# Macaron block on one core: attention and down weights loaded in parts, weight sums of the first block moved to GpSimd

## The chip, the cores and the metric

One core of a Trainium2 chip. The metric is the device time of one execution in microseconds (us); lower is better. Its engines are named as in the profile: PE (TensorE), DVE (VectorE), ACT (ScalarE), POOL (GpSimd) and SP (SyncE, which issues all DMAs of this kernel). A letter q behind an engine's name means its instruction queue.

## What is computed

The input `x` has 8 batches of 512 tokens of 512 features, all in float32. Each batch goes through a feed-forward stage, an attention stage and a second feed-forward stage with the same weights. The feed-forward stage keeps the two largest of every four hidden values.

```python
def _L0_ffn_ref(x, w_gate, w_up, w_down):
    h = silu(x @ w_gate) * (x @ w_up)      # 512 -> 2048
    h_sparse = _sparsify_2to4(h)           # two largest magnitudes of four stay
    return h_sparse @ w_down               # 2048 -> 512

x = x + 0.5 * _L0_ffn_ref(_layernorm(x), w_gate, w_up, w_down)
x = x + _L0_attn_ref(_layernorm(x), W_q, W_k, W_v, W_o)   # 16 heads, 4 of keys and values, rotary
x = x + 0.5 * _L0_ffn_ref(_layernorm(x), w_gate, w_up, w_down)
```

## The kernel before

**Blocks.** A block is one feed-forward stage of one batch; there are 16 of them, in an order that lets a batch's attention run beside the blocks of others. One block has four chunks of hidden values (`c`), each with two groups (`i`, 0 to 7). A group computes a quarter of a chunk's gate and up values.

**Products with sums of quarters.** A group's weights come as quarters of 256 KB: Q11, Q12, Q21, Q22. All groups but the first of the first block are done by seven products instead of eight (`woven`, L613 on): some take a quarter, others a sum of quarters S1 to S4 (S1 = Q21 + Q22, S2 = S1 - Q11, S3 = Q11 - Q21, S4 = Q12 - S2). The order in a group is Q11, S1, S2, S4, S3, Q12, Q22. The products that belong together collect in three PSUM banks x, v and z. ScalarE or VectorE copies what is there to `row` and `corner`; VectorE adds the later parts (L638), and a product into x must wait until VectorE has read x for `corner`. The last product of each group (`x<-ts,w`, Q22) is such a one: TensorE waits there if the add to `corner` is late.

**Sums of gate and up.** The sums do not change from block to block. The first block makes them (`combine_gu`, L688): for group i + 1 they are recorded after the third product of group i, four instructions on VectorE (L693) through a queue of work that may wait (`for_later`). Each sum is also stored to DRAM (L694), from where later blocks load it (L116).

**Mask.** After each chunk, VectorE makes the mask of two of four in two halves (`keep_two_of_four`, L393 on): L414, L416, L418, L419 compare magnitudes that ScalarE made (L401), eight bf16 steps L423 to L435 count, four L440 multiply the mask into `h`. GpSimd then makes sums of quarters of `h` (L446 after the first half; L448 to L451 after the second).

**Down.** Two chunks make a pair (`g`, 0 and 1). Each pair has seven products with the down weights (`products`, L532 on), in the order of the table PRODUCTS at L476: `11`, `11+12`, `22`, `21+22`, `11+22` and so on. Those that need sums of quarters of `w_down` load them from DRAM (L513), those that don't load from the input (L517). The sums are made in the first block by GpSimd (`combine_down`, L492 on): per chunk one load `raw` of 1 MB (L496), then five sums (L505), each stored (L506).

**Attention** (`attention`, L772 on) loads its weights `wqkv` (L776), the rotary tables `cs` (L780) and, later, `wo` (L830). It runs as a generator beside the feed-forward blocks: each `yield` is a step. It starts with `layernorm_t` (L278 on), which loads the rows `xn` (L286), makes their statistics on VectorE (L292), scales on GpSimd (L299 to L307), applies them on ScalarE (L310) and transposes on TensorE (L262).

**Order.** The program is written out in one order, and each engine carries out its own instructions in that order. A planner decides the order while the program is built: it keeps an estimated time for TensorE, VectorE and ScalarE (`at`), puts VectorE work that is not urgent where its estimate says that VectorE has room (`fill`), and advances the side stages (attention, layernorm, `combine_down`) when they are due by a table (`sides`, L1003): start, end, steps. GpSimd and the DMA queue have no estimate. All DMAs go through SP's queue, in order; a DMA that waits for an engine or for a free buffer holds those behind it. At most eight are under way: each waits for the eighth before it.

The lines that matter most:

```python
            raw = p_slots.tile([P, 4, D], FP, "raw")                       # L495
            nc.sync.dma_start(out=raw, in_=w_down[c])
            there = at["pe"] + 12.0
...
            def one(j, a, b, op):                                           # L692
                nc.vector.tensor_tensor(w[j], a, b, op)
                nc.sync.dma_start(out=gu_sums[i][:, j - S1], in_=w[j])
...
    sides = [(11, 18, 6, partial(combine_down, 0), None, None), (22, 32, 6, partial(combine_down, 1), None, None)]
```

Of the kernel before, what the change touches and what calls it, by code (L numbers as in the profile page):

```python
# [14 lines left out]
ALU = mybir.AluOpType  # L15
# [3 lines left out]
P = 128  # L19
# [7 lines left out]
def macaron_block(  # L27
# [12 lines left out]
    nc = tc.nc  # L40
    B, S, D = x.shape
    ND = D // P
    NT = S // P
    NCH = w_gu.shape[0]
    KV = N_KV * HD
# [27 lines left out]
    tokens = []  # L73
# [14 lines left out]
    Q11, Q12, Q22, Q21, S1, S2, S3, S4 = range(8)  # L88
# [52 lines left out]
    at = {"pe": 0.0, "dve": 0.0, "act": 0.0}  # L141
    urgent, put_off, for_later = deque(), deque(), deque()
# [33 lines left out]
    def waits(end):  # L176

        takes("pe", 0.0, end + TOLD)

    def later(us, does, ready=None, queue=put_off):  # L180
        queue.append(Later(us, does, pe_heard() if ready is None else ready, queue))
        return queue[-1]

    def soon(us, does, ready=None):

        return later(us, does, ready, urgent)
# [283 lines left out]
    gu_made, written = {}, {}  # L470
# [21 lines left out]
    def combine_down(g):  # L492

        for c in range(2 * g, 2 * g + 2):
            raw = p_slots.tile([P, 4, D], FP, "raw")  # L495
            nc.sync.dma_start(out=raw, in_=w_down[c])  # L496
            there = at["pe"] + 12.0
            yield lambda: there
            yield now
            quarter = {f"{i + 1}{j + 1}": raw[:, i::2, j * HD2 : (j + 1) * HD2] for i in range(2) for j in range(2)}  # L500
            sums = wa_slots.tile([P, 6, 2, HD2], FP, "sums")

            for i, name in enumerate(SUMS):
                op = ALU.add if name[2] == "+" else ALU.subtract
                nc.gpsimd.tensor_tensor(sums[:, i], quarter[name[:2]], quarter[name[3:]], op)  # L505
                nc.sync.dma_start(out=combined[g, name][:, c % 2 * 2 : c % 2 * 2 + 2, :], in_=sums[:, i])  # L506
            yield now
        done_down.add(g)
# [13 lines left out]
    def ffn(b, final, last):  # L522
# [165 lines left out]
        def combine_gu(i):  # L688

            w = [quarters[(b, final), i, q] for q in range(8)]  # L690

            def one(j, a, b, op):  # L692
                nc.vector.tensor_tensor(w[j], a, b, op)  # L693
                nc.sync.dma_start(out=gu_sums[i][:, j - S1], in_=w[j])  # L694

            gu_made[i] = [
                later(0.62, partial(one, j, w[a], w[b], op), at["pe"], for_later)
                for j, a, b, op in (
                    (S1, Q21, Q22, ALU.add),
                    (S2, S1, Q11, ALU.subtract),  # L700
                    (S3, Q11, Q21, ALU.subtract),
                    (S4, Q12, S2, ALU.subtract),
                )
            ]

        opens = (b, final) == blocks[0]
        hs, last_one = [], []
        for c in range(NCH):
# [27 lines left out]
            else:  # L736
                for pair in range(2):
                    i = 2 * c + pair
                    if opens and i == 0:
                        combine_gu(0)  # L740
                        groups = (g for r in range(2) for g in hidden(h, 0, r, slice(0, S)))
                        last_one = gu_made.pop(0)
                    else:
                        groups = woven(h, i, 2 * pair, last_one)
                    for k, g in enumerate(groups):
                        yield g
                        if k == 2 and opens and i + 1 < 2 * NCH:
                            combine_gu(i + 1)

                        if pair == 1 and c % 2 == 0 and k in (3, 4):  # L750
                            yield from some(1)
                    if opens:
                        load_quarters(*[key for key in quarters if key[:2] == ((b, final), i)])
                    if i == 2 * NCH - 1:
                        in_xT.remove(here)
                    if pair == 1:
                        begin(keep_two_of_four(h, list(last_one), e))
                        yield from some(5, False)
# [13 lines left out]
    def attention(b):  # L772
        ensure(written[b, 0])
        wa = wa_slots.tile([P, ND, D + 2 * KV], FP, "wqkv")
        for src, col in ((w_k, D), (w_q, 0), (w_v, D + KV)):
            nc.sync.dma_start(  # L776
                out=wa[:, :, col : col + src.shape[1]], in_=src.rearrange("(c p) n -> p c n", p=P)
            )
        cs = p_slots.tile([P, 4, S], FP, "cs")
        nc.sync.dma_start(out=cs[:, :2, :], in_=rope.rearrange("a p s -> p a s"))  # L780
        got = {}
        yield from layernorm_t(got, "xa", tokens[b][1])
        xT = got["xT"]
        qT = qkvp.tile([P, ND, S], FP, tag="qT", name="qT")
        kT = qkvp.tile([P, S], FP, tag="kT", name="kT")
# [29 lines left out]
        for t in range(NT):  # L815
            for k in range(ND):
                nc.tensor.matmul(  # L817
                    out=vps.tile[:, t, :],
# [8 lines left out]
        nc.scalar.copy(v, vps.tile)  # L827
        vps.free(end=takes("act", 0.6, pe_heard()))
        wo = wa_slots.tile([P, ND, D + 2 * KV], FP, "wo")
        nc.sync.dma_start(out=wo[:, :, :D], in_=w_o.rearrange("(c p) n -> p c n", p=P))  # L830
        yield partial(when, of_k + of_q[0])

        def scores(c, t, nm):

            sc = sc_slots.tile([P, N_KV, S], FP, "sc")
            waits(sc_slots.ready)
            for kv, rows in enumerate(heads):
                nc.tensor.matmul(  # L838
                    out=sc[:, kv, :], lhsT=qT[rows, c, t * P : (t + 1) * P], rhs=kT[rows, :], start=True, stop=True
                )  # L840
            multiplied(1.07, True)
            for kv in range(N_KV):
                one = partial(nc.vector.tensor_reduce, nm[:, t, kv : kv + 1], sc[:, kv, :], AX.X, ALU.max, negate=True)
                found = soon(0.6, one)
            return [sc_slots.used(found)]

        def in_pieces(nm):


            def pieces():  # L850
                nc.vector.tensor_copy(z[:, :, :, 0], nm)
                for i in (1, 2):
                    nc.vector.tensor_tensor(nm, nm, z[:, :, :, i - 1], ALU.subtract)
                    nc.vector.tensor_copy(z[:, :, :, i], nm)

            return [soon(1.15, pieces)]
# [63 lines left out]
        ensure(of_k + of_q[0])  # L920
        for t in range(NT):
            found = scores(0, t, nm)
            yield partial(when, found)
        pieces = in_pieces(nm)
        yield partial(when, pieces)
# [3 lines left out]
        p, sums = None, []  # L929
        for c in range(ND):  # L930
            waits(ensure(pieces))
            mT = pieces_by_row()
            there = [Done(at["act"])]
            nm = maxima()
            for t in range(NT):
# [15 lines left out]
                p = other if t else total  # L951
# [17 lines left out]
        for t, xt in enumerate(xts):  # L969
            y = Bank([P, D], "y")  # L970
            for k in range(ND):
                nc.tensor.matmul(  # L972
                    out=y.tile, lhsT=qT[:, k, t * P : (t + 1) * P], rhs=wo[:, k, :D], start=(k == 0), stop=(k == ND - 1)
# [26 lines left out]
        return WIDTH * blocks.index((b, i))  # L1000


    sides = [(11, 18, 6, partial(combine_down, 0), None, None), (22, 32, 6, partial(combine_down, 1), None, None)]  # L1003
    for b, i in blocks[1:]:
        stage = partial(layernorm_t, normed[b, i], "xf", tokens[b][2 * i])
        sides.append((place(b, i) - 15, place(b, i) - 2, NORM, stage, ("attention", b) if i else None, None))
    before = 0
    for b in range(B):

        left = place(B - 1, 1) - 13 - before  # L1010
        first = max(before, place(b, 0) + WIDTH + 16)
        if first % WIDTH > 17:
            first += WIDTH - first % WIDTH
        last = min(place(b, 1) - 13, max(before + left / (B - b), first + 1.4 * WIDTH))
        assert last - first > ATTENTION * 0.8
        sides.append((first, last, ATTENTION, partial(attention, b), ("attention", b - 1) if b else None, ("attention", b)))
        before = last
# [6 lines left out]
    n, running, past = 6.5, [], {None}  # L1024
# [22 lines left out]
    for b, i in blocks:  # L1047
# [71 lines left out]
```

## Time and profile before

| what | us |
|---|---|
| three runs | 3221.42, 3226.03, 3229.11 |
| median of the runs | 3226.03 |
| profiled execution | 3222.35 |
| its span, first to last instruction | 3220.5 |

The profile is of one execution. By stretches of the span (busy us of each engine in it; the first block ends near 160):

| stretch, us | PE | DVE | ACT | POOL | PE clock | DMA share |
|---|---|---|---|---|---|---|
| 0 to 27.7 | 19.79 | 15.21 | 7.30 | 0.69 | 1.00 | 0.57 |
| 27.7 to 62.4 | 34.70 | 21.10 | 9.69 | 13.14 | 1.00 | 0.76 |
| 62.4 to 70.4 | 3.30 | 8.00 | 0.00 | 2.32 | 0.79 | 0.71 |
| 70.4 to 123.2 | 49.71 | 48.79 | 11.27 | 30.61 | 1.00 | 0.80 |
| 123.2 to 160 | 36.80 | 26.82 | 14.67 | 11.46 | 1.00 | 0.63 |
| 123.2 to 3220 | 3072.60 | 2188.58 | 1153.78 | 561.35 | 1.00 | 0.42 |

In a line of the timeline, the first number is the start, the second how long the group of equal instructions took, then engine, source line, operation, what is written from what, shape and count; brackets hold the idle time of the engine just before, and what ended it.

### The profile page before, as it was taken

To read this page: it belongs to the slowest core of one execution; us is meant where nothing else is said; L and a number is where in the kernel's file an instruction comes from. 1 tells how busy PE (TensorE), PEld (TensorE's weight loads), DVE (VectorE), ACT (ScalarE), POOL (GpSimd) and SP (SyncE) were. 2 spreads that over 40 slices of the span, in tenths; PEclk is the share of its full clock that TensorE was granted. 3 is DMA by queue.
4 is the path that set the end of the run, shared out by engine and by line. 5 is a ranking of instruction groups with operands and counts; after the bars stand their busy time and mean duration, and the time that the engine had idled before them with its cause. 6 is when DMAs were issued, how large, how long until landed. Compare 5 with 4: busy or idle time off the path is not lost.

```text
span 3220.5 us, 43674 instructions
## 1 busy us (share of the span) xinstructions
PE 3180.1 (99%) x15880; PEld 2320.9 (72%) x15880; DVE 2281.7 (71%) x4869; ACT 1182.0 (37%) x1669; POOL 608.1 (19%) x888
## 2 busy tenths in 40 slices
PE   8999999999999999999999999999999999999999
PEld 6886668766776677767776668666776668666886
DVE  6867875678577775887578766678577775787554
ACT  2222552145324441354314532145324542255211
POOL 2422011211221112111121112111120122201120
PEclk9999999999999999999999999999999999999999
DMA  7762345433533434434543345333533446234451
GB/s 241 245 215 95 113 145 171 138 116 111 194 111 122 157 121 160 138 125 150 166 140 122 119 155 197 120 108 113 202 102 121 156 124 214 95 112 147 152 172 46
DMA packets 249285, 463.21 MB, mean 144 GB/s; under 512 B 24432, under 2 KB 64368, under 8 KB 248304
## 3 DMA queue, kind: packets, MB, share of 16 engines
q1 hardware_dynamic: 249072, 460.42, 43.3%
q8 instruction: 127, 2.08, 0.3%
q14 instruction: 86, 0.70, 0.1%
HBM read 421.53 MB, written 38.80 MB: 143 GB/s over the span
## 4 chain that ended last, share of the span: by engine, by line
PE 94%; DVE 3%; DMA 1%; ACT 1%; issue 0%; SPq 0%; DVEq 0%; ACTq 0%
PE x L624 26%; PE y L552 23%; PE v L624 13%; PE z L624 6%; PE proj L792 4%; PE sc L838 4%; PE st L871 4%; PE ops L887 4%; PE y L972 3%; PE tr L262 2%; PE gu L599 1%; PE den L903 1%; PE vps L817 1%; PE y L582 1%; PE st L876 1%; DMA xn<-x 1%
## 5 line engine op out<-in xcount | busy, mean ns | idle before, releaser
L624 PE MATMUL x<-ts,w 128*128 128x256 f32 x3000 | 720.2, 383 | 6.2 <-DVE corner L638 5.9
L624 PEld LDWEIGHTS x<-ts,w 128*128 128x128 f32 x3000 | 561.0, 190 | 151.4 <-issue 48.1
L552 PE MATMUL y<-wd,h 128*128 128x256 f32 x1984 | 455.2, 383 | 9.0 <-DVE h L440 6.4
L552 PEld LDWEIGHTS y<-wd,h 128*128 128x128 f32 x1984 | 372.8, 190 | 97.2 <-issue 28.8
L446 POOL TENSOR_TENSOR e<-h 128x512 f32<-128x512 f32 x62 | 96.6, 1559 | 1495.7 <-DVE h L440 1364.5
L164 DVE TENSOR_REDUCE nm<-sc 128x1 f32<-128x512 f32 x512 | 320.8, 683 | 63.5 <-PE sc L838 62.0
L565 DVE SCALAR_TENSOR_TENSOR x<-y,x 128x512 f32<-128x512 f32 x372 | 242.2, 686 | 135.6 <-PE y L552 133.8
L552 PE MATMUL y<-wd,e 128*128 128x256 f32 x1488 | 335.3, 380 | 1.0 <-PE den L903 1.0
L552 PEld LDWEIGHTS y<-wd,e 128*128 128x128 f32 x1488 | 281.3, 190 | 53.5 <-issue 11.0
L164 DVE TENSOR_TENSOR total<-total,p 128x512 f32<-128x512 f32 x384 | 266.2, 734 | 58.2 <-ACT p L879 58.2
L879 ACT ACTIVATE p<-st 128x2048 f32<-128x2048 f32 x96 | 179.6, 1870 | 283.2 <-PE st L876 191.3
L254 ACT ACT_TABLE_LOAD x206 | 264.3, 1283 | 4.4 <-PEq L1108 0.7
L673 ACT ACTIVATE h<-x 128x256 f32<-128x256 f32 x125 | 47.5, 380 | 592.8 <-PE x L624 573.1
L242 ACT COPY row<-x 128x512 f32<-128x512 f32 x210 | 122.9, 585 | 383.2 <-PE x L624 382.3
L624 PE MATMUL v<-ts,w 128*128 128x256 f32 x1000 | 238.8, 382 | 3.5 <-ACT xT L320 2.9
L624 PE MATMUL x<-xT,w 128*128 128x256 f32 x1000 | 239.8, 383 | 0.0
L624 PE MATMUL z<-xT,w 128*128 128x256 f32 x1000 | 239.4, 382 | 0.0
L624 PE MATMUL v<-xT,w 128*128 128x256 f32 x1000 | 239.0, 382 | 0.4 <-ACT corner L242 0.4
L624 PEld LDWEIGHTS x<-xT,w 128*128 128x128 f32 x1000 | 186.4, 190 | 50.8 <-issue 24.0
L624 PEld LDWEIGHTS v<-ts,w 128*128 128x128 f32 x1000 | 187.6, 190 | 46.9 <-issue 15.1
L624 PEld LDWEIGHTS z<-xT,w 128*128 128x128 f32 x1000 | 186.4, 190 | 48.2 <-issue 20.9
L624 PEld LDWEIGHTS v<-xT,w 128*128 128x128 f32 x1000 | 187.3, 190 | 45.5 <-issue 11.8
(109 smaller groups left out, 4114.0 us busy)
## 6 DMA issues: line engine op xcount, KB each, us to landing
w<-gu SPq DMA_DIRECT2D x472, 256.0 KB, 3.3
w<-in_w_gu SPq DMA_DIRECT2D x394, 256.0 KB, 3.3
wd<-wd SPq DMA_DIRECT2D x155, 512.0 KB, 3.8
wd<-in_w_down SPq DMA_DIRECT2D x124, 256.0 KB, 4.9
x<-x SPq DMA_DIRECT2D x64, 256.0 KB, 2.6
xn<-x SPq DMA_DIRECT2D x64, 256.0 KB, 6.9
x<-in_x SPq DMA_DIRECT2D x32, 256.0 KB, 3.4
gu<-w SPq DMA_DIRECT2D x32, 256.0 KB, 2.6
```

Source lines behind the costliest of these rows:

```text
L164: self.does()
L242: nc.scalar.copy(dst, src)
L254: nc.scalar.activation(dummy[:, 1:2], dummy[:, 0:1], f)
L552: nc.tensor.matmul(out=y.tile[:, t, :], lhsT=part[:, t * P : (t + 1) * P], rhs=operands[i][:, n, :], start=(n == 0), stop=(n == 3),)
L565: nc.vector.scalar_tensor_tensor(to, y.tile, 0.5 * sign, to, ALU.mult, ALU.add)
L624: nc.tensor.matmul(out=bank.tile[:, m, :], lhsT=lhs[:, m, k, :], rhs=rhs[:, k, :], start=(first and m == 0 and k == 0), stop=(k == 1), ski ...
L792: nc.tensor.matmul(out=ps.tile, lhsT=wa[:, k, col : col + P], rhs=xT[:, k, :], start=(k == 0), stop=(k == ND - 1))
L838: nc.tensor.matmul(out=sc[:, kv, :], lhsT=qT[rows, c, t * P : (t + 1) * P], rhs=kT[rows, :], start=True, stop=True)
L871: nc.tensor.matmul(out=st[:, kv, :], lhsT=kT[rows, t * P : (t + 1) * P], rhs=qT[rows, c, :], start=True, stop=False)
L879: nc.scalar.activation(p, st, AF.Exp)
L887: nc.tensor.matmul(out=ops[rows, :], lhsT=v[:, t, rows], rhs=p[:, kv, :], start=(t == 0), stop=(t == NT - 1))
L972: nc.tensor.matmul(out=y.tile, lhsT=qT[:, k, t * P : (t + 1) * P], rhs=wo[:, k, :D], start=(k == 0), stop=(k == ND - 1))
```

## The change

Three things change.

- `combine_down` loads `raw` in four parts of 256 KB, one in each of four steps, instead of 1 MB in one. It has ten steps instead of six for each pair, and the table `sides` starts the first earlier and ends both later.
- `combine_gu` makes the sums by GpSimd, at the place where it is called, instead of recording them for VectorE. The planner no longer counts time for them; it takes them as made 8 us later.
- `attention` issues the rows `xn` first. The weights for keys and values, the two rotary tables and four parts of the query weights follow, one with each step of `layernorm_t`. The output weights come in four parts beside the first four `scores` steps.

```diff
@@ combine_down
             raw = p_slots.tile([P, 4, D], FP, "raw")
-            nc.sync.dma_start(out=raw, in_=w_down[c])
-            there = at["pe"] + 12.0
-            yield lambda: there
-            yield now
+            for r in range(4):
+                nc.sync.dma_start(out=raw[:, r], in_=w_down[c][:, r])
+                there = at["pe"] + 5.0
+                yield now if r < 3 else lambda: there
@@ combine_gu
-            def one(j, a, b, op):
-                nc.vector.tensor_tensor(w[j], a, b, op)
+            for j, one, two, op in (
+                (S1, Q21, Q22, ALU.add),
+                (S2, S1, Q11, ALU.subtract),
+                (S3, Q11, Q21, ALU.subtract),
+                (S4, Q12, S2, ALU.subtract),
+            ):
+                nc.gpsimd.tensor_tensor(w[j], w[one], w[two], op)
                 nc.sync.dma_start(out=gu_sums[i][:, j - S1], in_=w[j])
-
-            gu_made[i] = [
-                later(0.62, partial(one, j, w[a], w[b], op), at["pe"], for_later)
...
-            ]
+            gu_made[i] = [Done(at["pe"] + 8.0)]
@@ attention
-        for src, col in ((w_k, D), (w_q, 0), (w_v, D + KV)):
-            nc.sync.dma_start(
-                out=wa[:, :, col : col + src.shape[1]], in_=src.rearrange("(c p) n -> p c n", p=P)
-            )
         cs = p_slots.tile([P, 4, S], FP, "cs")
-        nc.sync.dma_start(out=cs[:, :2, :], in_=rope.rearrange("a p s -> p a s"))
+        loads = deque()
+        for src, col in ((w_k, D), (w_v, D + KV)):
+            loads.append((wa[:, :, col : col + KV], src.rearrange("(c p) n -> p c n", p=P)))
+        for i in range(2):
+            loads.append((cs[:, i], rope[i]))
+        for k in range(ND):
+            loads.append((wa[:, k, :D], w_q[k * P : (k + 1) * P, :]))
         got = {}
-        yield from layernorm_t(got, "xa", tokens[b][1])
+        for ready in layernorm_t(got, "xa", tokens[b][1]):
+            if loads:
+                dst, src = loads.popleft()
+                nc.sync.dma_start(out=dst, in_=src)
+            yield ready
...
-        nc.sync.dma_start(out=wo[:, :, :D], in_=w_o.rearrange("(c p) n -> p c n", p=P))
...
             found = scores(0, t, nm)
+            nc.sync.dma_start(out=wo[:, t, :D], in_=w_o[t * P : (t + 1) * P, :])
@@ sides
-    sides = [(11, 18, 6, partial(combine_down, 0), None, None), (22, 32, 6, partial(combine_down, 1), None, None)]
+    sides = [(10, 19, 10, partial(combine_down, 0), None, None), (22, 34, 10, partial(combine_down, 1), None, None)]
```

More of the change, by code (lines that the diff above doesn't have):

```diff
@@ L690, in combine_gu @@
             w = [quarters[(b, final), i, q] for q in range(8)]
-            def one(j, a, b, op):
-                nc.vector.tensor_tensor(w[j], a, b, op)
-                nc.sync.dma_start(out=gu_sums[i][:, j - S1], in_=w[j])
-            gu_made[i] = [
-                later(0.62, partial(one, j, w[a], w[b], op), at["pe"], for_later)
[L698 to L702, printed above, removed]
-                )
-            ]
+            for j, one, two, op in (
[5 more added lines that the diff above has]
+                nc.gpsimd.tensor_tensor(w[j], w[one], w[two], op)
+                nc.sync.dma_start(out=gu_sums[i][:, j - S1], in_=w[j])
+            gu_made[i] = [Done(at["pe"] + 8.0)]
         opens = (b, final) == blocks[0]
@@ L774, in attention @@
         wa = wa_slots.tile([P, ND, D + 2 * KV], FP, "wqkv")
-        for src, col in ((w_k, D), (w_q, 0), (w_v, D + KV)):
-            nc.sync.dma_start(
-                out=wa[:, :, col : col + src.shape[1]], in_=src.rearrange("(c p) n -> p c n", p=P)
-            )
         cs = p_slots.tile([P, 4, S], FP, "cs")
-        nc.sync.dma_start(out=cs[:, :2, :], in_=rope.rearrange("a p s -> p a s"))
-        got = {}
-        yield from layernorm_t(got, "xa", tokens[b][1])
+        loads = deque()
[5 more added lines that the diff above has]
+            loads.append((wa[:, k, :D], w_q[k * P : (k + 1) * P, :]))
+        got = {}
+        for ready in layernorm_t(got, "xa", tokens[b][1]):
[3 more added lines that the diff above has]
+            yield ready
         xT = got["xT"]
```

## The prediction

> **What bounds the kernel now.** I read the shares of the engines first, then the waits of TensorE, then the timeline of the first block on TensorE, VectorE and GpSimd, then the loads there.
>
> ```profile
> PE 3180.1 (99%) x15880; PEld 2320.9 (72%) x15880; DVE 2281.7 (71%) x4869; ACT 1182.0 (37%) x1669; POOL 608.1 (19%) x888
> PE 94%; DVE 3%; DMA 1%; ACT 1%; issue 0%; SPq 0%; DVEq 0%; ACTq 0%
> ```
>
> TensorE is the bound. A change that leaves its instructions alone, as this one does (their order is the same in both programs), can only win or lose in its gaps: 3220.5 - 3180.1 = 40 us, of which 8 lie before the first product and 4 after the last. Of the rest, the largest stretch is in the first block. The next lines are the timeline of TensorE and of VectorE.
>
> ```profile
> 60.53 1.89 PE L624 MATMUL z<-xT,w 128*128 128x256 f32 x8
> 67.12 3.47 PE L624 MATMUL x<-ts,w 128*128 128x256 f32 x8 [4.70 <-DVE corner L638]
> ...
> 104.65 3.98 PE L552 MATMUL y<-wd,h 128*128 128x256 f32 x16 [1.55 <-issue]
> ...
> 116.25 7.15 PE L552 MATMUL y<-wd,h 128*128 128x256 f32 x32 [0.62 <-DMA wd<-wd]
> ```
>
> ```profile
> 55.65 0.69 DVE L414 TENSOR_TENSOR m<-a 128x512 bf16<-128x512 f32 x1
> 60.35 4.92 DVE L693 TENSOR_TENSOR w<-w 128x512 f32<-128x512 f32 x3 [4.01 <-DMA w<-in_w_gu]
> 65.19 0.68 DVE L638 TENSOR_TENSOR row<-v,row 128x512 f32<-128x512 f32 x1
> 65.79 0.68 DVE L693 TENSOR_TENSOR w<-w 128x512 f32<-128x512 f32 x1
> 66.39 0.68 DVE L638 TENSOR_TENSOR corner<-x,corner 128x512 f32<-128x512 f32 x1
> ```
>
> VectorE, in order, stood 4.01 us at sums whose weights had not landed, then spent 4.92 us on three of them, and the corner add that TensorE needed came 4.70 us late. The group that resumed took 3.30 us to the next (67.12 to 70.42) where others take 1.73: TensorE ran at half clock (the windows view has its clock at 0.79 from 62.4 to 70.4), 1.57 us more. These two, the small gaps at 81.29 (0.34), 92.04 (0.56), 104.65 and 116.25 and start delays put the start of group 6 at 123.23; back to back it were 27.72 + 7 x 12.08 = 112.3 (five groups of seven products of 1.726, and seven down products of 3.45 = 24.2, two groups' worth). So 10.9 us are lost here; nothing else in the span that a DMA causes is worth over 1 us.
>
> Why three VectorE sums took 4.92 instead of 2.0 is the key to this case. GpSimd was at work beside them:
>
> ```profile
> 57.67 7.05 POOL L505 TENSOR_TENSOR sums<-raw 128x512 f32<-128x512 f32 x5 [0.20 <-POOL e L446]
> ```
>
> ```profile
> 98.84 1.49 DVE L419 TENSOR_TENSOR m<-a 128x256 bf16<-128x256 f32 x1
> 100.25 1.35 DVE L423 TENSOR_TENSOR m<-m 128x256 bf16<-128x256 bf16 x1
> 101.52 0.28 DVE L424 TENSOR_TENSOR m<-m 128x256 bf16<-128x256 bf16 x1
> ```
>
> Beside the L505 of 94.01 to 101.45, a mask step of 0.42 takes 1.49 and one of 0.28 takes 1.35; the first after GpSimd has ended takes 0.28 again. Each such step waits for the end of one GpSimd instruction. Adds that read PSUM (L638) keep their 0.68.
>
> **What the Trainium skill says.** "SBUF — State Buffer", section Who interferes with whom: a VectorE instruction with two SBUF inputs and a GpSimd instruction that reads SBUF take the shared port in turn, and the later one fully blocks. The lines above agree (4.92 for three of 0.69). "GPSIMD Engine Reference", section 4.1 Engine selection: a two-input elementwise operation is about twice as slow there; here L505 takes 1.27 (its median) against 0.69 for L693. "TensorE: Matmul & The Clock Gate", What's actually happening: an idle window of about 3.4 us halves the clock until a busy window has passed; this trace's 3.30 for 1.73 agrees.
>
> **The change, part by part.**
>
> *Attention weights in parts (L774 on).* 8 stages; each 5 loads become 8, and `wo` 1 becomes 4. The bytes stay. Now the rows `xn` go ahead of the 2 MB. In the first attention `xn` takes 9.0 us to land and VectorE waits at its statistics; TensorE loses 0.79 at 220.74, and 0.27 at 2715.49. I book -1.0. Risk: parts of `w_q` stand behind loads that wait for TensorE. In program order the last part is 9.5 to 15.5 us of products ahead of its use (w_k 18 to 23, wo over 180); a 256 KB load lands in 3.3. No cost.
>
> *Down weights in quarters (L496).* 4 loads of 1 MB become 16 of 256 KB, spread over 10 steps instead of 6. SP is one queue in order, so their last quarter stands behind stores of sums: in the changed order, the fourth quarter of the first chunk follows the four stores of group 2, which wait for GpSimd.
>
> *Sums by GpSimd (L693).* VectorE loses 32 instructions, 0.69 alone (22 us in all, and its waits for DMA). GpSimd gains 32 x 1.27 = 41 us, of which some 36 fall before 105. While it works, every step of VectorE with two SBUF inputs (16 in each half of a chunk's mask, two for each group's `h`) costs about 1.4 us (bf16 and 256 wide) or 1.65 (512). And since the planner's VectorE is now empty, it puts the row and corner adds *behind* mask steps: the changed order has L423 to L427, row, L431 to L435, corner in group 2, and all of the second half's mask ahead of row and corner in group 3. I walk it:
>
> 1. Group 1's sums end at about 22.3 on GpSimd, group 2's loads follow, its sums end at 33.9, the fourth quarter of raw lands at 36.9, L505 runs to 43.7 (34.80 to 41.44 before). Group 3's sums: 43.7 to 49.9.
> 2. Mask half 0 begins at 45 (ScalarE's `a` waits for `h`, itself held by L505). L414, L416, L418, L419 pair with the four sums: 50.2. L423 to L427 0.9, row 0.6, L431 to L435 0.8, corner 0.65: 53.15. TensorE wants it at 50.17: **3.0 lost**.
> 3. L440 ends half 0 at 55.15. GpSimd then has L446, five L505 and group 4's four sums without a pause, to about 70. In these ten, ten steps of VectorE pair (L416, two of `h`, L418, L419, five bf16); the seven that are left and row and corner take 3.3: corner at 73.4. TensorE wants it at 62.26 + 3.0 = 65.3: **8.1 lost, and 1.6 at half clock**. Group 4 starts at 76.9 (70.42 before).
> 4. Group 4: corner 0.7 late. Group 5 starts at 76.9 + 12.08 + 0.7 = 89.7 (83.12 before). Seven products of 1.73 and four down products of 3.45 later, at 115.6, TensorE wants the weights of the fifth, `11+22`.
> 5. Its weights stand behind five stores, four `xn` and a quarter of raw. Group 5's second mask half ends at 101.2; GpSimd's L448 to L451 take 5.0, L505 5 x 1.27 and 0.8 of lock: last store at 113.4. Before, that load was issued 2.8 after the last store (101.48, 104.30) and landed 7.5 later, with 1 MB of raw ahead; 768 KB less at 0.66 per 256 KB saves 2.0. Landing: 113.4 + 2.8 + 5.5 = 121.7. **6.1 lost, and 1.6 at half clock.**
> 6. Group 6 starts at 121.7 + 3 x 3.45 + 1.6 = 133.7, against 123.23: **+10.5**. There GpSimd again has L505, the scales, L446 and group 7's sums (from about 142) beside a mask that stands ahead of row and corner: 0 to +4, I take 1.
>
> Sum: 10.5 + 1 - 1 = +10.5. The profiled execution, 3222.35 (span 3220.5 and 1.85 around it), would become 3232.9. The three runs of before have a median of 3226.03, 3.7 above it; on that base I forecast 3236. The unknown costs: a mask step in bf16 beside GpSimd is shown once (1.35); nothing shows L440 there. If neither is held, step 3's corner comes at 67.7; if both are, 73.4. Half clock is 0 or 1.6 each time. These two make the range from about +2 to +18.
>
> **Rivals.**
>
> *About even.* The lock holds only the fp32 steps. Then group 3 loses as much as before (corner 67.7 against 66.4), group 2 its 3.0, and the product for `11+22` is late by 3 instead of 6: +1 to +3, say 3228. For it: one line is all there is on bf16. Against: the rule is on inputs, not types.
>
> *Not slower.* VectorE keeps ahead because 32 instructions and the 4.0 us wait are gone, so the corner of group 3 is done before TensorE's 62.3. Then 6.4 us (4.87 and 1.57) come back at once and mask half 1 of group 5 ends near 86. GpSimd's last store is at 100.4, the weights for `11+22` land at 108.7 (111.9 before), which caps the gain at 3 to 4; with those in time too it is 10.9. With the loads of attention -4 to -11, 3218. For it: the wait at 60.35 does go, and loads are gated by earlier products now. Against: from 70.4 to 123.2 VectorE is busy 48.8 of 52.8 us already, and the 16 GpSimd sums of groups 3 to 6 (20 us at 1.27) hold 16 of its steps for about 1.1 us each, 18 us, while the same 16 sums took it 14.6 in L693 (2.70, 5.60, 3.59 and 2.71). It decides at the corner add of group 3: before or after 64 us.
>
> *The parts of attention come late.* If SP lags by ten us at `w_q` (then the distance is used up), each of 8 stages loses 1 to 2: 3242 to 3250. Against: the distances above. Were the SP queue so far behind, loads of quarters would stall TensorE today.
>
> **How the numbers follow.** Forecast 0.58, even 0.25, not slower 0.13, late attention 0.04. 0.2% (6.5 us) is about what the measurement can tell. Of the forecast all but a little is slower by more; of the even case 0.04 slower, the rest same; of the third 0.10 faster, 0.03 same. So faster 0.10, same 0.24, slower 0.66. The range for 8 in 10 runs from 3222 (leaving out the third) to 3245; the rest above is step 6 at its worst.
>
> **What would show it.** Right: TensorE idle before L624 near 50 to 53 and 65 to 74 by a DVE corner, VectorE's L418 to L440 at 1.3 to 1.5 us beside GpSimd, a wait on `wd` near 116, then group 6 after 130; no L693 on VectorE; the gap at 220 gone. Wrong: corner of group 3 before 64, short mask steps of 0.28 beside GpSimd, or group 6 before 122. A gap at L792 on `wqkv` would show the last rival.

## The result

| | before | after |
|---|---|---|
| median, us | 3225.46 (6 runs, 3221.42 to 3229.11) | 3247.73 (6 runs, 3244.18 to 3248.41) |
| ratio, 95% interval | | 1.0067 (1.0054 to 1.0080) |
| span of the profiled execution, us | 3220.5 | 3243.6 |

The changed kernel is slower by 22.3 us; 10.5 were forecast, and the range ended at 3245. The direction and most of the places were right, the size was not. From the page of the changed kernel, first the busy time of the engines, then the chain of waits by engine:

```profile
PE 3185.8 (98%) x15880; PEld 2323.7 (72%) x15880; DVE 2287.8 (71%) x4837; ACT 1181.6 (36%) x1669; POOL 647.1 (20%) x920
...
PE 94%; DVE 5%; ACT 1%; DMA 0%; issue 0%; DVEq 0%; ACTq 0%
```

GpSimd has 39.0 us more work. VectorE has 32 instructions fewer and yet 6.1 us more busy time: what it has left became longer. TensorE has the same instructions and is busy 5.7 us longer. The other 17 us or so are gaps. The timeline of TensorE of the changed kernel shows where (the last bracket of a line is the idle time before it and what ended it):

```profile
56.36 3.74 PE L624 MATMUL x<-ts,w 128*128 128x256 f32 x8 [5.98 <-DVE corner L638]
...
77.02 3.65 PE L624 MATMUL x<-ts,w 128*128 128x256 f32 x8 [6.57 <-DVE corner L638]
...
126.00 6.46 PE L552 MATMUL y<-wd,e 128*128 128x256 f32 x16 [5.97 <-DMA wd<-wd]
...
147.66 1.99 PE L624 MATMUL x<-ts,w 128*128 128x256 f32 x8 [1.39 <-ACT row L242]
...
155.51 3.66 PE L624 MATMUL z<-xT,w 128*128 128x256 f32 x8 [5.41 <-DVE row L638]
```

Before, one such gap stood in the first block, 4.70 at 67.12. Now there are four of 5.4 to 6.6, all before 160 us. After each of them the next group takes about 3.7 us instead of 1.9 (6.46 for 3.6 at 126.00), since the clock is at half. The view by stretches of the changed kernel (start:end, length, then busy time of PE, PEld, DVE, ACT and POOL, PE clock, DMA share, GB/s) has that clock in its column before the last two:

```profile
44.00:62.00 18.00, 12.02 (x48) 9.94 (x47) 17.04 (x23) 3.08 (x7) 12.71 (x10) 0.81 0.74 239
62.00:84.00 22.00, 15.44 (x65) 13.01 (x64) 18.09 (x22) 4.33 (x8) 18.84 (x15) 0.84 0.68 239
...
112.00:136.00 24.00, 18.03 (x72) 15.10 (x71) 12.76 (x20) 2.26 (x4) 10.29 (x18) 0.86 0.72 257
```

Between 44 and 62 TensorE worked 12.0 of 18 us and VectorE 17.0: for a short while VectorE is the bound. Its timeline in group 2 of the changed kernel, and GpSimd's beside it:

```profile
47.25 1.49 DVE L419 TENSOR_TENSOR m<-a 128x256 bf16<-128x256 f32 x1
48.66 1.36 DVE L423 TENSOR_TENSOR m<-m 128x256 bf16<-128x256 bf16 x1
49.94 1.35 DVE L424 TENSOR_TENSOR m<-m 128x256 bf16<-128x256 bf16 x1
51.21 0.28 DVE L426 TENSOR_TENSOR m<-m 128x256 bf16<-128x256 bf16 x1
51.41 1.34 DVE L427 TENSOR_TENSOR m<-m 128x256 bf16<-128x256 bf16 x1
52.68 0.68 DVE L638 TENSOR_TENSOR row<-v,row 128x512 f32<-128x512 f32 x1
...
55.62 0.68 DVE L638 TENSOR_TENSOR corner<-x,corner 128x512 f32<-128x512 f32 x1
```

```profile
42.41 7.45 POOL L505 TENSOR_TENSOR sums<-raw 128x512 f32<-128x512 f32 x5 [6.21 <-DMA raw<-in_w_down]
49.83 5.52 POOL L698 TENSOR_TENSOR w<-w 128x512 f32<-128x512 f32 x4
```

GpSimd works from 42.41 to 55.35 without a pause, nine instructions. In that time nine VectorE steps are held: seven in full (1.34 to 1.75 in place of 0.28 to 0.69) and two in part (0.88 at 43.35 and 0.74 at 53.28). Short ones slip in between (51.21). The add to `corner`, which TensorE needed at 50.4, stands behind twelve mask steps and comes at 55.62.

### The profile page after: what moved, and what is told of

It is laid out like the page before. It is cut to its first block, busy times and chain, and to the rows that moved or that the text cites. A ratio compares the mean times of both kernels' runs of the same rounds, so it can differ in the third digit from the quotient of the medians.

```text
span 3243.6 us, 43759 instructions
## 1 busy us (share of the span) xinstructions
PE 3185.8 (98%) x15880; PEld 2323.7 (72%) x15880; DVE 2287.8 (71%) x4837; ACT 1181.6 (36%) x1669; POOL 647.1 (20%) x920
## 4 chain that ended last, share of the span: by engine, by line
PE 94%; DVE 5%; ACT 1%; DMA 0%; issue 0%; DVEq 0%; ACTq 0%
PE x L624 26%; PE y L552 23%; PE v L624 13%; PE z L624 7%; PE proj L794 4%; PE sc L839 4%; PE st L872 4%; PE ops L888 4%; PE y L974 3%; PE tr L262 1%; PE gu L599 1%; PE den L904 1%; PE vps L819 1%; PE y L582 1%; PE st L877 1%; DVE total L164 0%
## 5 line engine op out<-in xcount | busy, mean ns | idle before, releaser
L446 POOL TENSOR_TENSOR e<-h 128x512 f32<-128x512 f32 x62 | 95.4, 1538 | 1488.9 <-DVE h L440 1365.4
```

## The experiments

The theory after the result was: GpSimd's sums read the same memory as VectorE's two-input steps and hold them; the adds to `row` and `corner` stand behind the held steps, so TensorE waits; the loads in parts matter little. Rivals: the quarter loads; the order of VectorE's work; the lateness of GpSimd's and SP's queues. Medians below are beside the runs of before on the same chip (3225.24 to 3225.80).

**The sums back on VectorE** (so the changed kernel with both kinds of loads in parts, but not the move).

```diff
-                nc.gpsimd.tensor_tensor(w[j], w[one], w[two], op)
+                nc.vector.tensor_tensor(w[j], a, b, op)
```

> The changed kernel with the sums of gate and up back on VectorE; both kinds of loads stay in parts. Theory (the sums on GpSimd hold VectorE's two-input steps): the loss goes, 3222 to 3228, no TensorE gap over 5 us beside group 2, group 3 or group 6. Rival (quarters of the down weights queued behind stores come late, the sums are harmless): still 3240 or more.

Measured: 3229.37 us, ratio 1.0013 (1.0006 to 1.0020). A little above what was expected; no gap of TensorE is over 3.8 once the first product has begun. Some 18 of the 22 us go with the move to GpSimd. The quarters of the down weights cost a little (5.6 us against the kernel with the attention parts alone, below): here L505 begins at 45.50, beside the sums of group 3 on VectorE (4.97 us for three), and `corner` is 3.6 us late.

**The move alone**, on the kernel before.

```diff
-                nc.vector.tensor_tensor(w[j], a, b, op)
+                nc.gpsimd.tensor_tensor(w[j], w[one], w[two], op)
```

> The kernel before with the sums of gate and up on GpSimd, nothing else changed. Theory: most of the loss is here, 3238 to 3250, with mask steps of 1.3 to 1.5 us beside GpSimd. Rival (loads): within 3 us of before, 3223 to 3229.

Measured: 3250.01 us, ratio 1.0075 (1.0060 to 1.0090), at the upper end of what was expected. The move is enough for the whole loss. But it does not lose it in the same places as the changed kernel. TensorE's timeline:

```profile
57.89 3.78 PE L624 MATMUL x<-ts,w 128*128 128x256 f32 x8 [6.02 <-DVE corner L638]
...
88.40 1.99 PE L624 MATMUL x<-ts,w 128*128 128x256 f32 x8 [3.76 <-DVE corner L638]
...
132.84 6.09 PE L552 MATMUL y<-wd,e 128*128 128x256 f32 x16 [13.04 <-DMA wd<-wd]
```

Group 2 loses what it loses in the changed kernel. Group 3 loses nothing (6.57 there), since the second L505 runs later, from 77.96, and holds the mask of group 4 (3.76). The weights of `11+22` are 13.04 late, not 5.97: ahead of that wait GpSimd stands 5.72 us at quarters that have not landed (105.75), with L448 to L451 and L505 behind.

**The attention loads alone**, on the kernel before (the diff of `attention` as above).

> The kernel before with the attention weights in parts, nothing else changed. Theory: TensorE's gaps of 0.79 at 220.74 and 0.43 at 2715.49 go, nothing else moves: about 1.2 us shorter, 3222 to 3226. Rival (query weights come late): 3230 or more and a wait of the projections on wqkv.

Measured: 3223.79 us, ratio 0.9998 (0.9989 to 1.0007): no difference that can be told. In its trace the two small gaps of attention are gone, as expected; a gap of 1.93 us at the weights of `11+22` (114.29) is new.

**One load of 1 MB again**, in the changed kernel, with the table `sides` of before.

```diff
-            for r in range(4):
-                nc.sync.dma_start(out=raw[:, r], in_=w_down[c][:, r])
+            nc.sync.dma_start(out=raw, in_=w_down[c])
```

> The changed kernel with the down weights again in one load of 1 MB for each chunk, six steps a pair. Theory: the raw rows land near 34 instead of 42, the first sums of down weights are over before the mask begins, group 2 loses 3 instead of 8: about 5 us below the changed kernel, 3240 to 3245, still slower than before. Rival (loads alone): all of the loss goes, 3223 to 3229.

Measured: 3248.11 us, ratio 1.0071 (1.0056 to 1.0086): the same total as the changed kernel, and the expectation missed. It had assumed that an early `raw` puts L505 ahead of the mask. GpSimd's timeline shows why not:

```profile
43.85 5.97 POOL L698 TENSOR_TENSOR w<-w 128x512 f32<-128x512 f32 x4 [8.88 <-DMA w<-in_w_gu]
49.79 6.65 POOL L505 TENSOR_TENSOR sums<-raw 128x512 f32<-128x512 f32 x5
```

`raw` had landed at 32.1, but L505 is recorded behind the sums of group 3, which wait for their quarters. The same nine instructions stand beside the same mask half, in the other order, and group 2's gap is 6.32 (5.98 with the quarters). For group 2, what counts is how many GpSimd instructions fall on the mask, not which. Past group 2 the equal totals are a coincidence: the gaps are those of the move alone, none at the corner of group 3, 3.78 at that of group 4, and 14.01 at `11+22`. So the loads in parts do decide where the loss falls, though here not how large it is.

**GpSimd without its reads.** Each sum becomes a sum of one column and two memsets. The sums of gate and up weights are left out, so S1 to S4 are zeros.

```diff
-                nc.gpsimd.tensor_tensor(w[j], w[one], w[two], op)
+                nc.gpsimd.tensor_tensor(w[j][:, 0, 0, 0:1], w[one][:, 0, 0, 0:1], w[two][:, 0, 0, 0:1], op)
+                nc.gpsimd.memset(w[j], 0.0)
+                nc.gpsimd.memset(w[j], 0.0)
```

> The changed kernel, but GpSimd reads almost nothing in the first block's gate-and-up sums: one column is summed and S1 to S4 are filled with zeros by two memsets (the sums themselves are left out, so the output is another). GpSimd keeps its place in the order, the waits for the quarter loads, and roughly the time it is occupied; the DMAs, TensorE's work and VectorE's order stay those of the changed kernel. Theory (GpSimd's reads hold VectorE's two-input steps): mask steps beside these memsets take 0.28 to 0.42 us; L505 still holds those that stand beside it. Group 2 then loses about 2 to 3 of its 6.0 us (half clock besides), group 3 about 2 of its 6.6, the product for 11+22 0 to 3 of its 6.0, group 6 0 to 3 of its 8.9: 3224 to 3234 us. Rival (it is the order, row and corner behind the mask, and the queue of GpSimd, not the reads): gaps as in the changed kernel, 3243 to 3250. If writes hold VectorE as reads do, also 3243 to 3250, but with mask steps of 1.3 beside the memsets.

Measured: 3239.07 us, ratio 1.0040 (1.0025 to 1.0055). The timelines of VectorE and GpSimd in group 2 (L698 is the small sum, L699 and L700 are the memsets):

```profile
49.27 1.36 DVE L423 TENSOR_TENSOR m<-m 128x256 bf16<-128x256 bf16 x1
50.55 0.28 DVE L424 TENSOR_TENSOR m<-m 128x256 bf16<-128x256 bf16 x1
50.76 0.28 DVE L426 TENSOR_TENSOR m<-m 128x256 bf16<-128x256 bf16 x1
50.96 0.28 DVE L427 TENSOR_TENSOR m<-m 128x256 bf16<-128x256 bf16 x1
51.16 0.68 DVE L638 TENSOR_TENSOR row<-v,row 128x512 f32<-128x512 f32 x1
...
52.56 0.68 DVE L638 TENSOR_TENSOR corner<-x,corner 128x512 f32<-128x512 f32 x1
```

```profile
43.04 7.44 POOL L505 TENSOR_TENSOR sums<-raw 128x512 f32<-128x512 f32 x5 [6.48 <-DMA raw<-in_w_down]
50.45 0.23 POOL L698 TENSOR_TENSOR w<-w 128x1 f32<-128x1 f32 x1
50.74 0.52 POOL L699 MEMSET w<- 128x512 f32 x1
51.32 0.52 POOL L700 MEMSET w<- 128x512 f32 x1
```

Until 50.48 L505 reads and the steps are held; from 50.45 on GpSimd is as busy as before, but writes, and the same kind of step takes 0.28. This is the Trainium skill, "SBUF — State Buffer", section Who interferes with whom: a two-input VectorE instruction contends with a GpSimd instruction that reads SBUF, not with one that only writes. The gap of group 2 fell from 5.98 to 2.57, and the one at the corner of group 3 went altogether. So the reads are the cause there, shown with the order of both engines unchanged. (Two memsets and the small sum take about 1.45 us together, a little more than the sum did.)

The sum of the expectation missed, however, by 5 us, for the product `11+22` became worse. TensorE's and GpSimd's timelines:

```profile
125.55 5.27 PE L552 MATMUL y<-wd,e 128*128 128x256 f32 x16 [12.14 <-DMA wd<-wd]
```

```profile
90.65 1.26 POOL L446 TENSOR_TENSOR e<-h 128x512 f32<-128x512 f32 x1
99.09 0.19 POOL L698 TENSOR_TENSOR w<-w 128x1 f32<-128x1 f32 x1 [7.18 <-DMA w<-in_w_gu]
...
109.86 6.34 POOL L505 TENSOR_TENSOR sums<-raw 128x512 f32<-128x512 f32 x5
```

TensorE arrives earlier (113.4, not 120.0), but the weights for `11+22` land at 125.4, as in the changed kernel (125.9). GpSimd stood idle for 7.18 us at sums whose quarters had not landed, with L448 to L451 and L505 behind. This is a second cause, which the first had covered in the changed kernel; in the move alone, and with one load, it shows beside the first.

**That second cause: stores on GpSimd's own queue.** As the last kernel (sums left out), but the stores of the sums no longer stand on SP's queue, where each waited for GpSimd and held the next group's loads.

```diff
-                nc.sync.dma_start(out=gu_sums[i][:, j - S1], in_=w[j])
+                nc.gpsimd.dma_start(out=gu_sums[i][:, j - S1], in_=w[j])
```

> The kernel whose first-block sums are memsets on GpSimd (sums left out, so the output is another), with their stores issued from GpSimd's own DMA queue as against SP's, where each store waits for GpSimd and holds the loads behind it. Theory (what was left without the reads, 12.1 us at the product for 11+22, is a ring: loads of quarters behind stores on SP, stores behind sums on GpSimd, sums behind loads): the quarter loads of group 6 are issued some 3.6 us earlier, GpSimd's wait of 7.2 us at 99 and its last L505 come forward by as much, the gap falls from 12.1 to 5 to 8, and the waits of TensorE for sums at 75 and 90.7 (0.8 and 2.3) shrink: 3229 to 3235 us. Rival (GpSimd's order alone: L448 to L451 and L505 stand behind sums whose quarters come late, whatever queue): 12 us stay, 3238 to 3241. If issuing from GpSimd costs it over 1 us each, later than 3240.

Measured: 3233.43 us, ratio 1.0022 (1.0015 to 1.0029), as the theory had it (the gap is slightly over the 5 to 8 expected). The two intervals touch (this one ends at 1.0029, that of the last kernel begins at 1.0025), so the traces have to show the gain. GpSimd's and TensorE's timelines:

```profile
87.29 1.28 POOL L446 TENSOR_TENSOR e<-h 128x512 f32<-128x512 f32 x1
88.51 0.26 POOL L698 TENSOR_TENSOR w<-w 128x1 f32<-128x1 f32 x1
88.83 0.52 POOL L699 MEMSET w<- 128x512 f32 x1
...
90.23 0.58 POOL L701 DMA_DIRECT2D gu<-w  x1 [0.30 <-POOL w L700]
...
102.76 6.16 POOL L505 TENSOR_TENSOR sums<-raw 128x512 f32<-128x512 f32 x5
```

```profile
118.32 4.18 PE L552 MATMUL y<-wd,e 128*128 128x256 f32 x9 [8.83 <-DMA wd<-wd]
```

The wait of 7.18 us is gone and L505 comes 7.1 us earlier. That was a ring: loads behind stores on SP, stores behind sums on GpSimd, sums behind loads. It was broken here with the sums left out; how much of the waits of 5.97, 13.04 and 14.01 it explains, with the sums in, was not tried. The 8.83 us that stay are left to GpSimd's order: L505 stands behind L448 to L451, where before it stood ahead of them (L505 at 94.01, L448 from 106.23). That last part was read from the traces and not tried by itself. (A gap of 3.08 came back at the corner of group 3, where L505 now falls on the second mask half.)

**VectorE's order of before**, sums on GpSimd at the planner's place for them, with their 0.62 us still booked.

```diff
-                nc.gpsimd.tensor_tensor(w[j], w[one], w[two], op)
...
+                nc.gpsimd.tensor_tensor(w[j], a, b, op)
...
+                later(0.62, partial(one, j, w[a], w[b], op), at["pe"], for_later)
```

> The changed kernel, its sums still on GpSimd, but issued when the planner would have run them on VectorE, and with their 0.62 us still booked on VectorE: so VectorE's order is that of the kernel before, with row and corner of groups 2 to 4 ahead of most of the mask, as against behind it. Theory (held steps cost, and the order only decides where they hit): the gaps at the corners of groups 2 and 3 shrink to under 3 us each, but the held steps (some 30 of them, about 1 us each) are still to be done; they come late at group 4 to 6, at the mask that the down products need and at the down weights: 3236 to 3244 us, a third to a half of the loss back. Rival A (the order is the whole cause): 3222 to 3230. Rival B (the lag of GpSimd's queue is the whole cause, VectorE's order does nothing): 3244 to 3250.

Measured: 3237.45 us, ratio 1.0038 (1.0023 to 1.0053), as the theory had it. The corners of groups 2 and 3 now come in time (50.19 and 62.82), but the held steps remain, as VectorE's timeline shows:

```profile
62.82 0.69 DVE L638 TENSOR_TENSOR corner<-x,corner 128x512 f32<-128x512 f32 x1 [0.96 <-PE x L624]
...
66.89 1.35 DVE L423 TENSOR_TENSOR m<-m 128x256 bf16<-128x256 bf16 x1
68.17 1.35 DVE L424 TENSOR_TENSOR m<-m 128x256 bf16<-128x256 bf16 x1
```

The loss moves to group 4 (gaps of 2.73 and 3.15 near 70 and 80), to the down products (1.93 and 3.61 at 102 and 112) and to group 6 (2.24 and 2.32). The order is worth some 10 us (VectorE's, and with it the place of the sums and stores on GpSimd and SP, which the edit moves too); it does not remove the cause. With the stores on GpSimd's queue as well:

```diff
                 nc.gpsimd.tensor_tensor(w[j], a, b, op)
-                nc.sync.dma_start(out=gu_sums[i][:, j - S1], in_=w[j])
+                nc.gpsimd.dma_start(out=gu_sums[i][:, j - S1], in_=w[j])
```

> The changed kernel with the VectorE order of the kernel before (sums on GpSimd, issued where the planner would have run them on VectorE) and the stores of these sums from GpSimd's own DMA queue. Theory (ring of SP and GpSimd, and held steps): the 3237.5 us of the same order with stores on SP fall by 2 to 6, to 3231 to 3236, since the quarters at 96.7 (GpSimd waits 8.8 us for them) come earlier; the held steps keep it above the kernel before. Rival (SP's queue does nothing): 3236 to 3239.

Measured: 3234.98 us, ratio 1.0027 (1.0020 to 1.0033); the interval overlaps with the last one, so the gain of 2.5 is not settled.

**The last group's sums on VectorE**, the others on GpSimd.

```diff
+                if i == 2 * NCH - 1:
+                    made.append(later(0.62, partial(run, nc.vector), at["pe"], for_later))
+                else:
+                    run()
```

> The changed kernel, with the four gate-and-up sums of the last group (7) alone back on VectorE. Theory (in step 6 the sums of group 7 on GpSimd hold the mask of chunk 2 and so the corner, the row copy and xn): up to 132 us the same gaps as the changed kernel, then group 6's 8.9 us (1.4 at 147.7, 5.4 at 155.5, 1.8 at half clock) shrink to 0 to 3; end 6 to 9 us earlier: 3238 to 3242 us. Rival (L505 and the scales on GpSimd hold it, not these four): the gap at 155.5 stays over 4: 3245 to 3249.

Measured: 3240.88 us, ratio 1.0046 (1.0029 to 1.0062), as the theory had it. TensorE's timeline in group 6:

```profile
150.09 1.99 PE L624 MATMUL x<-ts,w 128*128 128x256 f32 x8 [1.26 <-ACT row L242]
...
154.31 1.99 PE L624 MATMUL z<-xT,w 128*128 128x256 f32 x8 [1.78 <-DVE row L638]
```

5.41 became 1.78, and the half clock after it is gone: four sums, 5.3 us of GpSimd, had cost 5 to 7 us at the end. The 1.3 at `row` stay, so they come from elsewhere.

**Is there a better kernel?** Three tries, all with the attention weights in parts, the down weights in loads of 1 MB and the sums on VectorE. First, the planner is told that the sums can be made 4 us later, so that VectorE does not stand at quarters that are still under way.

```diff
-                later(0.62, partial(one, j, w[a], w[b], op), at["pe"], for_later)
+                later(0.62, partial(one, j, w[a], w[b], op), at["pe"] + 4.0, for_later)
```

> The kernel before, with the attention weights in parts, the down weights in single loads of 1 MB and the sums on VectorE; the planner is told that each group's sums can be made 4 us later than before, so that row and corner adds stand ahead of sums whose weights have not landed. Theory (what the kernel before loses in the first block is VectorE standing at L693 for a DMA): the 4.7 us gap at the corner of group 3 and the 1.6 at half clock go; the rest is capped by the down weights near 116: 3217 to 3222 us. Rival (the stall only moves, since mask half 0 now stands ahead of the corner of group 3 and beside L505): a gap of 3 to 6 us stays in group 3 or 4: 3223 to 3230.

Measured: 3226.98 us, ratio 1.0006 (0.9998 to 1.0015). The rival holds: a gap of 5.62 at the corner of group 3, which now stands behind mask steps beside L505. Second, the same for group 4 alone, and the planner counts the second mask half of the first chunk at 1 to 2 us more per step (`slow` is 1.0 there, else 0).

```diff
+                ... at["pe"] + (4.0 if i == 4 else 0.0) ...
-            yield 0.72, 0.0
+            yield 0.72 + slow, 0.0
```

> The kernel before with the attention weights in parts, the sums on VectorE, and two things told to the planner: the sums of group 4 can be made 4 us later (their quarters have not landed), and the second mask half of the first chunk costs VectorE its time beside GpSimd's L505 (1 to 2 us more per step). Row and corner of group 3 then stand ahead of both. Theory (the kernel before loses its 4.7 us because VectorE stands at a DMA and then behind L505): that gap and the 1.6 at half clock go, the down weights near 116 cap the gain: 3217 to 3221 us. Rival (it moves to group 4, whose last two sums now stand behind the mask): a gap of over 3 us near 70: 3222 to 3226.

Measured: 3222.92 us, ratio 0.9991 (0.9984 to 0.9997). The corner of group 3 is in time; a gap of 5.20 moved to 74.71, where a copy to `corner` stands behind the mask: the rival's price, though not its instruction. Third, from the kernel of before with the attention parts, the second `raw` of 1 MB is issued behind the quarters of group 4 instead of ahead of them (the first pair of chunks then has seven steps in `sides`, not six).

```diff
         for c in range(2 * g, 2 * g + 2):
+            if c == 1:
+                room = at["pe"] + 4.0
+                yield lambda: room
```

> The kernel before with the attention weights in parts; the sums stay on VectorE and the down weights come in single loads of 1 MB, but the second of these loads is issued behind the four quarter loads of group 4, as against ahead of them. VectorE's order is not changed. Theory (the 4 us for which VectorE stands at L693 near 60 are the time that 1 MB takes on the queues ahead of the quarters, and L505 then runs beside those sums for the same reason): the quarters land near 55 us and not at 58.8 to 60.7, L693 waits less than 1 us and takes 0.69 each, the corner of group 3 is in time, the gap of 4.5 to 4.7 us and the half clock go; the product for 11+22 near 116 then caps the gain, or L505 (now near 61 to 68) beside the mask gives 1 to 3 us back: 3216 to 3221 us. Rival (L505, later by some 3.5 us, holds the second mask half, and group 4 loses as much as group 3 did): a gap of over 3 us between 64 and 84, 3221 to 3227.

Measured: 3221.98 us, ratio 0.9988 (0.9980 to 0.9996). VectorE's and TensorE's timelines (lines stand three further down in this kernel):

```profile
60.06 2.02 DVE L696 TENSOR_TENSOR w<-w 128x512 f32<-128x512 f32 x3 [3.34 <-DMA w<-in_w_gu]
```

```profile
63.94 1.99 PE L627 MATMUL x<-ts,w 128*128 128x256 f32 x8 [1.14 <-DVE corner L641]
...
76.39 2.79 PE L627 MATMUL x<-ts,w 128*128 128x256 f32 x8 [3.55 <-ACT row L242]
```

The three sums take 2.02 us where they took 4.92 beside L505, and the gap of 4.70 is 1.14. The quarters still land at 57.3 to 60.0, only 0.8 to 1.5 us earlier than in the kernel with the attention parts alone, so most of the wait remains: the 1 MB ahead of them was not what made them late, and the theory was wrong in that. The rival holds: the later L505 holds the second mask half, what VectorE and ScalarE do after it is late, and 3.55 us are lost in group 4. The last two versions are about 0.1% below the kernel before.

## Why the prediction was right, and where it failed

The lag of each start behind the kernel before, from the two profiled executions, gives the bookkeeping:

| step of the prediction | forecast, us | measured, us |
|---|---|---|
| 2, corner of group 2 | 3.0 | 6.0 + 1.9 at half clock |
| 3, corner of group 3 (the whole gap) | 8.1 + 1.6 | 6.6 + 1.8 |
| 4, corner of group 4 | 0.7 | 0.7 |
| 5, wait for the weights of `11+22` | 6.1 + 1.6 | 6.0 + 2.9 |
| group 6 starts later by | 10.5 | 139.20 - 123.23 = 16.0 |
| 6, after that | 1 | 1.6 + 5.6 + 1.8 = 9.0 |
| attention | -1.0 | -0.8 - 0.4 = -1.2 |
| end | 10.5 | 3243.6 - 3220.5 = 23.1 |

The kernel before lost 4.7 + 1.6 of its own at step 3 and, beyond what the changed kernel loses likewise, 3.6 in small gaps and late starts up to group 6. These go off the lag: 25.9 - 6.3 - 3.6 = 16.0. From group 6 to the end 0.7 are given back in small gaps. The direction was right; the size failed at steps 1 and 2 and at step 6.

*Steps 1 and 2 failed in one term.* "the fourth quarter of raw lands at 36.9, L505 runs to 43.7": it was issued at 36.60 and landed at 42.25, and L505 ran from 42.41 to 49.86. Two things made it late: the sums of group 2, whose stores stand ahead of it on SP, ended at 36.21 and not at 33.9, and the load took 5.65 us to land, where the median for a 256 KB quarter is 3.3 (`w<-in_w_gu`). So the mask of group 2 stood beside nine GpSimd instructions and not beside the four sums: 6.0 us lost in place of 3.0. Half clock was counted at steps 3 and 5 and not here, but it followed this gap too: another 1.9. These 4.9 are nearly the whole excess of 5.5 at group 6. The experiment with one load shows that the late quarter was not the cause as such: with `raw` there ten us earlier, L505 falls on the same mask from the other side.

*Step 3 was right in its mechanism.* "Ten steps pair" was the unknown that made the range; the bf16 steps are held like the fp32 ones. The half clock was 1.8. A corner at 73.4 was forecast; it came at 76.29, with group 3 itself 4.9 later than forecast, so the gap was 1.5 smaller. Forecast was a GpSimd without a pause from 55.15 on; in fact it stood 2.17 us before L505, which began at 61.75, and in that time L416 and one step of `h` ran at their own length. (The start of group 4 at 76.9 is also 0.2 above the sum of the terms: 70.42 + 3.0 + 8.1 + 1.6 - 6.4 is 76.7.)

*Steps 4 and 5 were right in the wait, step 5 with some luck.* The weights landed 4.2 us later than forecast (125.9, not 121.7), and TensorE arrived 4.4 later, so the wait was the same; the half clock behind it cost 2.9, not 1.6. What was not seen is a second cause behind it, the ring of SP and GpSimd: without the reads, the weights land at the same time and the wait is 12.1. In the move alone and with one load, the wait is 13.04 and 14.01.

*Step 6 failed: "0 to +4, I take 1" was 9.0.* Forecast was that something stands there; the value was taken without walking it. From 146.26 to 152.96 GpSimd has L446 and the four sums of group 7, five VectorE steps of mask half 1 take 1.35 each, and row and corner of group 6 stand behind the whole of it. GpSimd's and VectorE's timelines of the changed kernel:

```profile
146.26 1.41 POOL L446 TENSOR_TENSOR e<-h 128x512 f32<-128x512 f32 x1
147.63 5.33 POOL L698 TENSOR_TENSOR w<-w 128x512 f32<-128x512 f32 x4
```

```profile
146.46 1.35 DVE L423 TENSOR_TENSOR m<-m 128x256 bf16<-128x256 bf16 x1
...
154.78 0.68 DVE L638 TENSOR_TENSOR row<-v,row 128x512 f32<-128x512 f32 x1
```

The same walk as for group 2 would have given it. The kernel with these four sums on VectorE shows that they are worth 5 to 7.

*The rivals.* "About even", in which only fp32 steps are held, is out: bf16 steps at 1.34 to 1.36 stand all along. "Not slower" decided at a corner add of group 3 before or after 64 us: it came at 76.29. "Attention late" is out: no product waits on `wqkv`.

## What to carry to other kernels

Work moved from VectorE to GpSimd is not taken away from VectorE if it reads SBUF beside two-input steps of VectorE: in the changed kernel each such instruction held about one VectorE step for some 1.1 us, even a step of 0.28, so a mask of short steps was a bad neighbour. Ask for each stage what stands beside the moved work and what stands behind that on the same engine, and walk every stage in which both occur, the last one too. Compare variants gap by gap: two kernels with the same total lost it in different places here. And where a load, a store and a sum wait for each other over two in-order queues, look for the ring; another cause can cover it.

## What the runs showed of the hardware

- In the changed kernel a VectorE step was mostly held by one GpSimd instruction at a time: 0.28 became 1.35, 0.42 became 1.49, and 0.69 became 1.75, that is, some 1.07 us more, a little less than the 1.27 us of a GpSimd sum. Of the mask steps 256 wide that began inside a GpSimd sum there, none kept its length.
- It was not always one. In the two kernels whose stores stand on GpSimd's queue, single VectorE steps were held through four or five GpSimd instructions: 5.92 us (103.56) and 5.41 (148.75) without the reads, and 5.36 (103.02) for a step of 0.42 in the order of before. No other kernel has a VectorE step over 1.95 us; the cause stays open.
- It can go the other way. In the move alone, a GpSimd sum that began at 65.22 took 3.62 us, while VectorE's short steps beside it kept their 0.28 and 0.42; with one load, one took 3.39.
- The multiply of the mask (L440, a `scalar_tensor_tensor`), which the prediction had left open, can be held as well: 1.81 us for two at 145.34, in the kernel with VectorE's order of before, in place of 0.75.
- After gaps of 6 us TensorE's next group of eight took 3.7 instead of 1.9 us. The Trainium skill's page "TensorE: Matmul & The Clock Gate", section What's actually happening, has a window of about 3.4 us of idle time after which the clock halves. Gaps of 5 to 14 us agree: they cost 1.7 to 3.1 each in what followed. Shorter ones don't sort by length: without the reads a gap of 2.57 was followed by a group of 3.47, and in the move alone a gap of 3.76 by one of 1.99.
- A store issued by GpSimd takes 0.57 us of its time, with 0.30 idle before it. In the order of before with the stores there, VectorE got two steps of 0.28 through in such a pause (69.05 and 69.25); the next, begun while the store was issued, took 1.82.
